# Count digits of a graph kernel stored in the order in which PE reads them

## The chip, the cores and the metric

The kernel runs on one core of a Trainium2 chip. The metric is the device time of one execution in microseconds (us). The engines are PE (matrix products; its weight loads are listed as PEld), DVE (vector), ACT (scalar), POOL (GpSimd) and SP, which here only issues DMAs. Each engine works through its own queue in order; marks on semaphores make one queue wait for another.

## The reference

Four graph layers over 8192 nodes of 32 features and 262144 edges, each followed by a residual and a layer norm. The edges come sorted by their target node `dst`.

```python
src = src[argsort(dst)]; dst = dst[argsort(dst)]
x = layernorm(x + segment_sum(einsum(x[src], weight[edge_type]), dst))   # 64 relations, 32 x 32 each
x = layernorm(x + segment_sum(x[src] * edge_weight[:, None], dst))
x = layernorm(x + segment_sum(x[src], dst))
x = layernorm(x + L3(x, src, dst, edge_attr_4, edge_attr_32, W1, b1, W2, b2, si_w0, si_w1))
```

Nothing in the reference counts edges. The kernel counts them because layers two and three work on matrices that are built from the edges of each node, and for that it has to find where each node's edges begin.

## The kernel before, in words

**Layout.** The 262144 edges stand as 2048 tiles of 128 edges, one edge per partition, so every per-edge array is 128 x 2048 (`TT` = 2048). Eight tiles (`GT` = 8) make a group; there are 256 groups (`GG`). The targets of a group lie in a window of 128 nodes that moves by 32 nodes per group, and `rel` is an edge's target within its window, 0 to 127.

**The first stage** (up to about 320 us) does two things at once. One is the table `ytab`: every node's features times all 64 relation matrices, 64 MB in memory. The loop at L391 makes it in 64 steps. A step is eight products on PE (L402), two copies out of the PSUM banks (L408, both on ACT at first, later one on ACT and one on DVE) and one store of 1 MB issued by SP (L410). Five buffers `ys` take turns, so a copy waits for the store of five steps ago.

The other thing is the start of every node's edges, in the generator `beginnings()` (L280). Each table step first advances the generator to its next `yield`, so the order of the queues is: what the generator issues, then the step's own table work. The generator runs as follows.

1. At its first turn it issues all digit work to DVE. L285 takes the target's position in the window, L286 to L289 split it into a low digit (0 to 15, `lo_b`) and a high digit (0 to 7, `hi_b`), both bf16 in the order of the edges: group, then tile within the group. L291 to L293 are checks and the conversion of `rel`. L296 makes the one-hot low digits `oh_lo`, one instruction for each of 16 values, stored as value x 2048 edges. L300 makes the one-hot high digits `oh_hi`, in two halves of eight instructions each; a mark `begun[h]` stands behind each half.
2. For 20 turns it does nothing, so 20 table steps are queued on PE.
3. In each of the next eight turns it queues count products for two blocks of 16 groups (L315 to L324). For each block and each of the eight tile positions `t`, one product multiplies the one-hot high digits of 16 groups (the weights, 128 columns: group x digit) with their one-hot low digits (the moving operand, 256 columns: digit x group), and the eight add up in PSUM bank 6. Only the parts in which both groups are the same are wanted: DVE multiplies with `mask` (L323) and sums over the group (L324). PE waits for `begun[0]` at the first turn, for `begun[1]` at the fifth, and at every turn for L324 of the turn before, since the bank is the same.
4. The counts are stored to `hist` (L327), read back shifted (L333), added up over the four windows in which a node can lie, and summed into running totals (L336 to L354).
5. POOL gathers 64 times the records of the edges with these totals as indices (the indirect DMAs of `laid_rec`).

**What follows.** POOL's gathers of `ytab` for the first layer wait for all stores of the table. Then come the first layer with the building of the matrices (to about 4835 us), the second and third layers, which read these matrices back (to about 5900 us), and the fourth layer.

**The lines of the change.** The moving operand is a view of `oh_lo` that takes, for a fixed tile position `t`, all 16 values and all 16 groups: from one column to the next the address moves by eight bf16 elements, 16 bytes, and from one value to the next by 2048 elements. The weights are a gapless run.

Of the kernel before, what the change touches and what calls it, by code (L numbers as in the profile page):

```python
# [13 lines left out]
BF = mybir.dt.bfloat16  # L14
I32 = mybir.dt.int32
AF = mybir.ActivationFunctionType
OP = mybir.AluOpType
# [4 lines left out]
P = 128  # L22
# [11 lines left out]
TT = E // P  # L34
GT = 8
# [110 lines left out]
def raw_layers(tc, x, a, w0, w1, b1, w2, si, m, bad):  # L146
    nc = tc.nc
    PE, V, A, G, S = (Flow(tc, e, n) for e, n in ((nc.tensor, "pe"), (nc.vector, "dve"), (nc.scalar, "act"),
                                                  (nc.gpsimd, "pool"), (nc.sync, "sp")))
    bank, arena = m["bank"], m["arena"]  # L150
# [33 lines left out]
    def own(f, ins):  # L184

        mk = f.mark(ins)
        f.after(mk)
        return mk
# [3 lines left out]
    cut = Carve()  # L192
# [13 lines left out]
    cut = Carve(8192)  # L206
    rg = cut(64, MS, 3)
    rgi = rg.rearrange("p a b c -> p (a b c)").bitcast(I32).rearrange("p (a b c) -> p a b c", b=MS, c=3)
    cut = Carve(8192)
    nxt = cut(TT, dt=I32)  # L210
    base = cut(GG, GT, dt=I32)
    cut = Carve()
    oh_lo = cut(16, TT, dt=BF)
    oh_hi = [cut(8, GT, 16, 8, dt=BF)]
    dg = cut
    dg4, pre, idx, idx2 = dg(4, 64), dg(2, 64), dg(64, dt=I32), dg(64, dt=I32)
    NY = 5
    ys = cut(NY, 4, 512)
    w0_s = cut(R * D)
    xT = cut(NB // 4, P)  # L220
    oh_hi.append(cut(8, GT, 16, 8, dt=BF))
    mask = cut(16, 16)
    c16 = cut(16, 16)
    ev = cut(2, 16, 16)
# [3 lines left out]
    hi_b = digits[:, 0:TT // 2].bitcast(BF)  # L228
    lo_b = digits[:, TT // 2:TT].bitcast(BF)
# [48 lines left out]
    begun = {}  # L278

    def beginnings():  # L280


        bf, xi = base.rearrange("p g t -> p (g t)"), x_a.rearrange("p d f -> p (d f)").bitcast(I32)
        V.after(dst_in, g2)
        own(V, V.e.tensor_tensor(bf, dsti, bf, op=OP.subtract))  # L285
        own(V, V.e.tensor_scalar(xi, bf, 15, None, op0=OP.bitwise_and))  # L286
        own(V, V.e.tensor_copy(lo_b, xi))
        own(V, V.e.tensor_scalar(xi, bf, 4, None, op0=OP.arith_shift_right))
        V.e.tensor_copy(hi_b, xi)  # L289
        V.after(nxt_in)  # L290
        own(V, V.e.tensor_tensor(nxt, dsti, nxt, op=OP.is_gt))  # L291
        V.e.tensor_reduce(ok[:, 2:3], nxt, AX.X, OP.max)
        own(V, V.e.tensor_copy(rel, bf))  # L293

        for c in range(16):
            V.e.tensor_scalar(oh_lo[:, c, :], lo_b, float(c), None, op0=OP.is_equal)  # L296
        for h in range(2):
            for k in range(8):
                t0 = 1024 * h + 128 * k
                ins = V.e.tensor_tensor(oh_hi[h][:, k].rearrange("p t g c -> p g t c"),  # L300
                                        m["iota_b"][:, None, None, 0:8].to_broadcast([P, 16, GT, 8]),
                                        hi_b[:, t0:t0 + 128].rearrange("p (g t) -> p g t", t=GT)[:, :, :, None].to_broadcast([P, 16, GT, 8]),
                                        op=OP.is_equal)
            begun[h] = V.mark(ins)
        S.after(zm)
        h_ld = Landing(tc, "st_hist")
        for g in (0, GG + 2):
            h_ld.add(S.e.dma_start(hist[g:g + 2].rearrange("g h c -> (g h) c"), z[0:8, 0:32].rearrange("p (h c) -> p h c", c=16)))
        for _ in range(20):
            yield  # L310
        V.after(g4)
        counts = bank[:, 6, :].rearrange("p (h c g) -> p h c g", h=2, g=16)
        cm = None
        for k in range(8):
            PE.after(begun[k // 4], cm)  # L315
            for h in range(2):
                n = 2 * k + h
                lv = oh_lo[:, :, 128 * n:128 * (n + 1)].rearrange("p c (g t) -> p c g t", t=GT)
                for t in range(GT):
                    ins = PE.e.matmul(counts[:, h], oh_hi[n // 8][:, n % 8, t].rearrange("p g c -> p (g c)"), lv[:, :, :, t],  # L320
                                      start=(t == 0), stop=(t == GT - 1))
            V.after(PE.mark(ins))
            own(V, V.e.tensor_tensor(ev, counts, mask[:, None].to_broadcast([P, 2, 16, 16]), op=OP.mult))  # L323
            cm = own(V, V.e.tensor_reduce(c16[:, 2 * k:2 * k + 2, :], ev, AX.X, OP.add))  # L324
            yield
        S.after(cm)
        hm = h_ld.add(S.e.dma_start(hist[2:GG + 2].rearrange("(s g) h c -> (g h) s c", s=16), c16))  # L327
        yield
        S.after(hm)
        d_ld = Landing(tc, "ld_deg")  # L330
        for i in range(4):
            v = hist[i:i + GG, 2 * (3 - i):2 * (3 - i) + 2, :].rearrange("(p b) h c -> p b (h c)", b=2)
            dm = d_ld.add(S.e.dma_start(dg4[:, i, :].rearrange("p (b n) -> p b n", b=2), v))  # L333
        yield
        V.after(dm)
        own(V, V.e.tensor_add(dg4[:, 0:2, :], dg4[:, 0:2, :], dg4[:, 2:4, :]))  # L336
        own(V, V.e.tensor_add(dg4[:, 2, :], dg4[:, 0, :], dg4[:, 1, :]))
        deg = dg4[:, 2, :]
        own(V, V.e.tensor_copy(pre[:, 0, :], deg))
        k = 1  # L340
        f = 0
        while k < 64:
            V.e.tensor_copy(pre[:, 1 - f, 0:k], pre[:, f, 0:k])
            own(V, V.e.tensor_add(pre[:, 1 - f, k:], pre[:, f, k:], pre[:, f, 0:64 - k]))
            k *= 2
            f = 1 - f
        vm = own(V, V.e.tensor_sub(pre[:, 1 - f, :], pre[:, f, :], deg))
        PE.after(vm, g3, cm)
        pm = PE.mark(PE.e.matmul(bank[:, 6, 0:1], upper, pre[:, f, 63:64], start=True, stop=True))
        V.after(pm)  # L350
        own(V, V.e.tensor_copy(small[:, 7:8], bank[:, 6, 0:1]))
        own(V, V.e.tensor_scalar(idx, pre[:, 1 - f, :], small[:, 7:8], None, op0=OP.add))
        own(V, V.e.tensor_scalar(idx2, idx, RG - 1, None, op0=OP.bitwise_and))
        im = own(V, V.e.tensor_scalar(idx, idx, RG.bit_length() - 1, None, op0=OP.arith_shift_right))  # L354

        G.after(im)
        r_ld = Landing(tc, "ld_rec")
        for k in range(64):
            begun["rec"] = r_ld.add(indirect(rg[:, k].rearrange("p s f -> p (s f)"), a["rec"], idx[:, k:k + 1]))
        yield  # L360

        own(V, V.e.tensor_tensor(pre[:, f, :], idx2, deg, op=OP.add))
        own(V, V.e.tensor_reduce(ok[:, 3:4], pre[:, f, :], AX.X, OP.max))
        V.after(src_in, row_in)
        begun["row"] = own(V, V.e.scalar_tensor_tensor(row, src, float(R), row, op0=OP.mult, op1=OP.add))
        V.e.tensor_reduce(ok[:, 0:1], rel, AX.X, OP.max)
        own(V, V.e.tensor_reduce(ok[:, 1:2], rel, AX.X, OP.min))
        own(V, V.e.tensor_scalar(ok[:, 0:1], ok[:, 0:1], float(P - 1), None, op0=OP.is_gt))
        own(V, V.e.tensor_scalar(ok[:, 1:2], ok[:, 1:2], 0.0, ok[:, 0:1], op0=OP.is_lt, op1=OP.max))
        own(V, V.e.tensor_scalar(ok[:, 2:3], ok[:, 2:3], 0.0, ok[:, 1:2], op0=OP.is_gt, op1=OP.max))  # L370
        om = V.mark(V.e.tensor_scalar(ok[:, 3:4], ok[:, 3:4], float(MS), ok[:, 2:3], op0=OP.is_gt, op1=OP.max))
        yield
        yield
        yield
        PE.after(om)
        pm = PE.mark(PE.e.matmul(bank[0:1, 6, 8:9], ok[:, 3:4], small[:, 1:2], start=True, stop=True))
        V.after(pm)
        own(V, V.e.tensor_copy(bad, bank[0:1, 6, 8:9]))
# [9 lines left out]
    n = 0  # L388
    rest = beginnings()
    busy = True  # L390
    for j in range(NB // 4):  # L391
        for c in range(4):
# [4 lines left out]
            for h in range(2):  # L397
# [3 lines left out]
                for q in (2 * h, 2 * h + 1):  # L401
                    ins = PE.e.matmul(bank[:, 2 * b + q % 2, :], xT[q * D:(q + 1) * D, j, :],  # L402
                                      w0_s[q * D:(q + 1) * D, c * 512:(c + 1) * 512], start=True, stop=True)
# [187 lines left out]
    for s in range(NS):  # L591
        if s == FIRST - 1:
            V.after(slots(), x_in)
        k, landed = gathers(ytab, row, s)
        g0 = s * WT // GT
        for h in range(2):
# [3 lines left out]
            for t in range(16):  # L600
                g = (s * WT + 16 * h + t) // GT
                bk = (g // per) % 2
                if t % GT == 0 and g % per == 0:
                    PE.after(agg_free[bk])
                c = g % per
                ins = PE.e.matmul(bank[:, bk, c * D:(c + 1) * D], oh[:, h, t, :], xg[:, k, 16 * h + t, :],  # L606
                                  start=(t % GT == 0), stop=(t % GT == GT - 1))
# [20 lines left out]
    cut = Carve()  # L628
# [47 lines left out]
    for n, (l, c) in enumerate(seq):  # L676
# [8 lines left out]
        for s in range(64):  # L685
            if l == 1:
                q = s % 4
                ins = PE.e.matmul(bank[q * D:(q + 1) * D, b, 0:256].rearrange("p (u h j) -> p u h j", h=2, j=4),  # L688
                                  x_b[:, s, :], mv[:, s], start=(s < 4), stop=(s >= 60), tile_position=(0, q * D))
            else:  # L690
                ins = PE.e.matmul(bank[0:96, b, 0:512].rearrange("p (u h j) -> p u h j", h=2, j=4),  # L691
                                  x3[:, s, :], mv[:, s], start=(s == 0), stop=(s == 63))
# [13 lines left out]
    cut = Carve()  # L706
# [20 lines left out]
    p = cut(NP, 4, MW)  # L727
# [110 lines left out]
    for q in range(NQ + 4):  # L838
# [3 lines left out]
        if q < NQ:  # L842
            k, wp = w_bank()
# [5 lines left out]
        c = q - 3  # L849
        if 0 <= c < NQ:  # L850
            g = c // 2
# [14 lines left out]
        ins = None  # L866
        if 0 <= q - 2 < NQ:
            c = q - 2
# [38 lines left out]
        c = q - 3  # L907
# [486 lines left out]
```

## Time and profile before

| what | us |
|---|---|
| median of three timed runs | 9409.51 |
| lowest and highest of them | 9387.47, 9425.49 |
| the profiled execution | 9317.46 |
| its span, first to last instruction | 9315.7 |
| PE busy, PE weight loads busy | 5952.4, 4149.0 |
| DVE, ACT, POOL busy | 3749.4, 1626.5, 3971.2 |
| count products L320, 128 of them, in a stage of | 75.0 |
| DVE: digits, from L285 to the end of L300 | 16.5 to 57.4 |

The shares of busy time are averages over stages with different limits. A weight load can run beside a product, so the two PE rows don't add up. [...]for the count products the start-to-start time is what counts, and it is read from the timeline. The granted clock is the share of its full rate that PE's throttle left it.

### The profile page before, as it was taken

The numbers are of one execution on the slowest core, as the hardware profiler recorded it, in microseconds if no ns is written. First come the engines' busy times: TensorE is split into PE (matmuls) and PEld (weight loads), VectorE is DVE, ScalarE is ACT, GpSimd is POOL, SyncE is SP. The second block draws the span as 40 slices with busy tenths as digits, with TensorE's granted clock in tenths as the row PEclk, the third lists the DMA queues.
The fourth block names the chain that finished last, engine by engine and source line by source line (L and its number), as shares of the span: only waits on it lengthen the run. The fifth ranks groups of instructions, "written<-read, shape, count | busy, mean of one in ns | idle before, by whom it ended". The sixth has DMA issues, their size and how long they took to land.

```text
span 9315.7 us, 88230 instructions
## 1 busy us (share of the span) xinstructions
PE 5952.4 (64%) x36084; PEld 4149.0 (45%) x36084; DVE 3749.4 (40%) x6576; ACT 1626.5 (17%) x2828; POOL 3971.2 (43%) x4174
## 2 busy tenths in 40 slices
PE   6325444544545445444464467399989988999899
PEld 2124444434445445444452234155555555555555
DVE  3213333333334333333330000166666665666666
ACT  3122222222222222222230000011111111111111
POOL 2554443443444444444400000655655555555551
PEclk6556666666666666666677778599998888989899
DMA  6304333333333333333369999011111110111110
GB/s 229 126 21 104 96 90 107 112 90 115 103 92 120 97 100 112 96 101 112 96 206 432 430 414 371 19 24 21 24 21 23 21 23 20 21 23 21 23 21 15
DMA packets 290653, 999.43 MB, mean 107 GB/s; under 512 B 98941, under 2 KB 175806, under 8 KB 250558
## 3 DMA queue, kind: packets, MB, share of 16 engines
q1 hardware_dynamic: 155662, 916.89, 27.3%
q0 software_dynamic: 134144, 73.67, 5.6%
q8 instruction: 285, 4.67, 0.2%
q10 hardware_dynamic: 432, 3.15, 0.1%
q14 instruction: 130, 1.06, 0.0%
HBM read 521.39 MB, written 471.99 MB: 107 GB/s over the span
## 4 chain that ended last, share of the span: by engine, by line
PE 38%; another core or an unknown queue 34%; DMA 15%; ACT 5%; issue 4%; DVE 3%; SPq 0%; ACTq 0%; DVEq 0%
PE bank L854 12%; PE bank L846 8%; DMA fcmat<-f_arena 7%; PE bank L828 5%; DMA f_arena<-famat 5%; PE bank L567 5%; PE bank L606 2%; DMA f_arena<-fcmat 2%; ACT f_arena L571 2%; ACT f_arena L572 2%; PE bank L688 2%; PE bank L691 1%; DVE f_arena L889 1%; PE bank L402 1%
## 5 line engine op out<-in xcount | busy, mean ns | idle before, releaser
L381 POOL DMA_INDIRECT f_arena<-fxtab,f_src x2048 | 1943.0, 949 | 2523.4 <-DMA fxtab<-f_x_b 1172.4
L381 POOL DMA_INDIRECT f_arena<-fytab,f_row x2048 | 1960.9, 957 | 2465.5 <-PE bank L606 1774.0
L567 PE MATMUL bank<-f_arena 64*128 64x128 f32 x16384 | 1382.4, 333 | 2109.5 <-ACT f_arena L572 1651.1
L567 PEld LDWEIGHTS bank<-f_arena 64*128 64x128 f32 x16384 | 1273.1, 238 | 2212.2 <-ACT f_arena L572 1667.5
L854 PE MATMUL bank<-f_arena 128*128 128x344 f32 x4096 | 1439.1, 498 | 165.7 <-DVE f_arena L501 127.1
L553 DVE TENSOR_TENSOR f_arena<-bank,f_arena 128x1024 f32<-128x1024 f32 x256 | 312.4, 1220 | 2557.9 <-PE bank L567 2490.5
L571 ACT ACTIVATE f_arena<-bank 128x512 bf16<-128x512 f32 x1024 | 612.9, 598 | 2928.0 <-remote 2204.8
L854 PEld LDWEIGHTS bank<-f_arena 128*128 128x128 f32 x4096 | 851.3, 210 | 602.0 <-DVE f_arena L501 157.4
L846 PE MATMUL bank<-f_arena 65*128 65x256 f32 x4096 | 1091.7, 412 | 0.0
L846 PEld LDWEIGHTS bank<-f_arena 65*128 65x128 f32 x4096 | 775.6, 199 | 538.2 <-issue 440.6
L833 ACT ACTIVATE f_arena<-bank,f_arena 64x512 f32<-64x512 f32 x512 | 350.3, 684 | 2913.2 <-PE bank L828 1475.6
L606 PE MATMUL bank<-f_arena 128*128 128x32 f32 x4096 | 686.9, 340 | 111.8 <-DMA f_arena<-fytab,f_row 59.6
L501 DVE TENSOR_TENSOR f_arena<-bank,f_rel 128x512 f32<-128x512 f32 (+1 forms) x640 | 634.5, 999 | 263.9 <-ACT f_arena L533 240.1
L606 PEld LDWEIGHTS bank<-f_arena 128*128 128x128 f32 x4096 | 679.9, 264 | 121.1 <-issue 115.5
L828 PE MATMUL bank<-f_arena 32*64 32x512 f32 x1024 | 577.4, 644 | 188.5 <-ACT f_arena L833 179.1
L572 ACT ACTIVATE f_arena<-bank 128x512 f32<-128x512 f32 x1024 | 611.3, 597 | 0.0
L882 DVE TENSOR_TENSOR f_arena<-bank,f_arena 128x256 f32<-128x256 f32 x512 | 216.1, 422 | 937.1 <-PE bank L846 379.1
L555 DVE TENSOR_TENSOR f_arena<-bank,f_arena 128x2048 f32<-128x2048 f32 x256 | 586.5, 2291 | 8.8
L889 DVE TENSOR_TENSOR f_arena<-bank,f_arena 128x256 f32<-128x256 f32 x1536 | 550.6, 414 | 0.0
L688 PE MATMUL bank<-f_arena,f_x_b 128*32 128x256 f32 x4096 | 295.5, 459 | 336.4 <-DMA f_arena<-famat 336.4
L688 PEld LDWEIGHTS bank<-f_arena,f_x_b 128*32 128x32 f32 x4096 | 145.6, 132 | 475.0 <-DMA f_arena<-famat 311.4
L885 DVE TENSOR_TENSOR f_arena<-bank,f_arena 128x512 f32<-128x512 f32 x512 | 348.6, 681 | 0.0
(127 smaller groups left out, 2711.9 us busy)
## 6 DMA issues: line engine op xcount, KB each, us to landing
famat<-f_arena SPq DMA_DIRECT2D x256, 1024.0 KB
fcmat<-f_arena SPq DMA_DIRECT2D x256, 512.0 KB
fytab<-f_arena SPq DMA_DIRECT2D x64, 1024.0 KB
f_arena<-fytab,f_row POOLq DMA_INDIRECT x2048
f_arena<-fxtab,f_src POOLq DMA_INDIRECT x2048
f_arena<-laid_ea SPq DMA_DIRECT2D x64, 512.0 KB
f_arena<-laid_ea SPq DMA_DIRECT2D x64, 64.0 KB
f_arena<-laid_xT ACTq DMA_DIRECT2D x1, 1024.0 KB, 8.3
```

Source lines behind the costliest of these rows:

```text
L381: return G.e.indirect_dma_start(out=dest, out_offset=None, in_=table, in_offset=bass.IndirectOffsetOnAxis(ap=ix, axis=0))
L501: return V.e.tensor_tensor(o, iota[:, None, :].to_broadcast([P, n, P]), rel[:, t:t + n, None].to_broadcast([P, n, P]), op=OP.is_equal)
L555: V.e.tensor_tensor(oh_l[:, b], iota[:, None, :].to_broadcast([P, 16, P]), meta_l[:, pp, k0:k0 + 16, None].to_broadcast([P, 16, P]), op=OP ...
L567: ins = PE.e.matmul(bank[:, bk + h, :].rearrange("p (c s j) -> p c s j", s=64, j=4)[:, :, :, j], oh_l[hs_, b, 4 * q + j, :], oh_k[hs_, b, ...
L571: A.e.activation(st_c[:, b, q], bank[:, bk:bk + 2, 0:256], AF.Copy)
L572: bank_free[units[0] % 2] = am = A.mark(A.e.activation(st_a[:, b, q], bank[:, bk:bk + 2, 256:512], AF.Copy))
L606: ins = PE.e.matmul(bank[:, bk, c * D:(c + 1) * D], oh[:, h, t, :], xg[:, k, 16 * h + t, :], start=(t % GT == 0), stop=(t % GT == GT - 1))
L688: ins = PE.e.matmul(bank[q * D:(q + 1) * D, b, 0:256].rearrange("p (u h j) -> p u h j", h=2, j=4), x_b[:, s, :], mv[:, s], start=(s < 4), ...
L828: pm = PE.mark(PE.e.matmul(bank[0:64, 2, :], w1_s[r * D:(r + 1) * D, :], ef[r * D:(r + 1) * D, k, (q % 8) // 4, :], start=True, stop=True))
L846: ins = PE.e.matmul(wp[:, t, :], hs[0:65, q % 3, t * P:(t + 1) * P], w2_s[0:65], start=True, stop=True)
L854: ins = PE.e.matmul(bank[:, g % 2, 0:MW], oh[:, c % NO, t, :], p[:, c % NP, t, :], start=(c % 2 == 0 and t == 0), stop=(c % 2 == 1 and t = ...
L889: V.e.tensor_tensor(pq[:, :, 128 + 64 * mm:192 + 64 * mm].rearrange("p t (o i) -> p t o i", i=8), wp[:, :, 192:256].rearrange("p t (o i) - ...
```

## The change

The order of the digits is changed where they are made, so that the count products read gapless runs. The casts of L287 and L289 write the digits in the order block of 16 groups, tile position, group, and read their int32 source with a step of eight elements to do so. `oh_lo` becomes (block and tile position) x value x group, so that each of the 16 comparisons writes 128 runs of 16 elements. `oh_hi` becomes (block and tile position) x group x digit, written gapless by one instruction per half in place of eight. The count products take one block of `oh_lo` and one of `oh_hi` at a time; their results stand in the bank as before, and L323's view of them is renamed accordingly. The sizes of the buffers, the marks and the order of the queues stay.

```diff
-    oh_lo = cut(16, TT, dt=BF)
-    oh_hi = [cut(8, GT, 16, 8, dt=BF)]
+    oh_lo = cut(16 * GT, 16, 16, dt=BF)
+    oh_hi = [cut(8 * GT, 16, 8, dt=BF)]
...
-    oh_hi.append(cut(8, GT, 16, 8, dt=BF))
+    oh_hi.append(cut(8 * GT, 16, 8, dt=BF))
...
-        own(V, V.e.tensor_copy(lo_b, xi))
+        own(V, V.e.tensor_copy(lo_b.rearrange("p (n t g) -> p n t g", t=GT, g=16),
+                               xi.rearrange("p (n g t) -> p n t g", t=GT, g=16)))
         own(V, V.e.tensor_scalar(xi, bf, 4, None, op0=OP.arith_shift_right))
-        V.e.tensor_copy(hi_b, xi)
+        V.e.tensor_copy(hi_b.rearrange("p (n t g) -> p n t g", t=GT, g=16),
+                        xi.rearrange("p (n g t) -> p n t g", t=GT, g=16))
...
         for c in range(16):
-            V.e.tensor_scalar(oh_lo[:, c, :], lo_b, float(c), None, op0=OP.is_equal)
+            V.e.tensor_scalar(oh_lo[:, :, c, :], lo_b.rearrange("p (k g) -> p k g", g=16), float(c), None, op0=OP.is_equal)
         for h in range(2):
-            for k in range(8):
-                t0 = 1024 * h + 128 * k
-                ins = V.e.tensor_tensor(oh_hi[h][:, k].rearrange("p t g c -> p g t c"),
-                                        m["iota_b"][:, None, None, 0:8].to_broadcast([P, 16, GT, 8]),
-                                        hi_b[:, t0:t0 + 128].rearrange("p (g t) -> p g t", t=GT)[:, :, :, None].to_broadcast([P, 16, GT, 8]),
-                                        op=OP.is_equal)
-            begun[h] = V.mark(ins)
+            n = 1024
+            begun[h] = V.mark(V.e.tensor_tensor(oh_hi[h].rearrange("p k g c -> p (k g) c"),
+                                                m["iota_b"][:, None, 0:8].to_broadcast([P, n, 8]),
+                                                hi_b[:, n * h:n * (h + 1), None].to_broadcast([P, n, 8]), op=OP.is_equal))
...
-        counts = bank[:, 6, :].rearrange("p (h c g) -> p h c g", h=2, g=16)
+        counts = bank[:, 6, :].rearrange("p (h n) -> p h n", h=2)
...
-                lv = oh_lo[:, :, 128 * n:128 * (n + 1)].rearrange("p c (g t) -> p c g t", t=GT)
                 for t in range(GT):
-                    ins = PE.e.matmul(counts[:, h], oh_hi[n // 8][:, n % 8, t].rearrange("p g c -> p (g c)"), lv[:, :, :, t],
+                    ins = PE.e.matmul(counts[:, h], oh_hi[n // 8][:, n % 8 * GT + t].rearrange("p g c -> p (g c)"),
+                                      oh_lo[:, n * GT + t].rearrange("p c g -> p (c g)"),
                                       start=(t == 0), stop=(t == GT - 1))
...
-            own(V, V.e.tensor_tensor(ev, counts, mask[:, None].to_broadcast([P, 2, 16, 16]), op=OP.mult))
+            own(V, V.e.tensor_tensor(ev, counts.rearrange("p h (c g) -> p h c g", g=16), mask[:, None].to_broadcast([P, 2, 16, 16]), op=OP.mult))
```

## The prediction, made before the changed kernel was run

> **What bounds the kernel now.** The change lies in the first 320 us, so I cut that stretch into stages with the view by windows (columns: stretch, its length, busy us of PE, PE's weight loads, DVE, ACT, POOL, granted clock, DMA share, GB/s):
>
> ```profile
> 17.00:64.50 47.50, 45.92 (x160) 16.56 (x152) 40.20 (x40) 36.54 (x39) 0.00 (x0) 0.72 1.03 392
> 64.50:139.50 75.00, 75.00 (x196) 20.04 (x196) 11.02 (x16) 15.27 (x16) 0.00 (x0) 0.50 0.44 162
> 139.50:166.00 26.50, 15.48 (x64) 6.28 (x58) 11.62 (x30) 13.24 (x14) 7.13 (x7) 0.59 0.62 201
> 166.00:248.00 82.00, 25.25 (x60) 6.22 (x56) 7.69 (x7) 7.58 (x9) 54.68 (x58) 0.53 0.54 182
> 248.00:318.00 70.00, 51.76 (x176) 18.50 (x176) 28.97 (x25) 23.27 (x23) 0.00 (x0) 0.57 1.00 362
> ```
>
> Before 64.5 us and after 248 us the stores of the table `ytab` fill the DMA engines (share 1.0). Between 64.5 and 139.5 us they don't (0.44, 162 GB/s): PE is busy without a gap, at half clock. That is the stage of the count products. The timeline shows one step of it:
>
> ```profile
> 64.58 7.41 PE L320 MATMUL bank<-f_arena 128*128 128x256 bf16 x16
> 71.92 2.09 PE L402 MATMUL bank<-f_arena 32*128 32x512 f32 x8
> 72.09 0.69 DVE L323 TENSOR_TENSOR f_arena<-bank,f_arena 128x512 f32<-128x512 f32 x1 [14.69 <-PE bank L320]
> 72.82 0.69 DVE L324 TENSOR_REDUCE f_arena<-f_arena 128x32 f32<-128x512 f32 x1
> 73.94 7.41 PE L320 MATMUL bank<-f_arena 128*128 128x256 bf16 x16
> ```
>
> From 64.58 to 73.94 a step takes 9.36 us: 16 count products (7.34 us, 0.459 each) and one step of the table (2.02 us). Eight of them are 74.9 us. Last, the chain of waits and the timeline say what hangs on their end:
>
> ```profile
> 141.98 5.43 DMA fhist<-f_arena
> 149.83 2.20 DMA f_arena<-fhist
> ```
> ```profile
> 157.04 1.10 POOL L381 DMA_INDIRECT f_arena<-laid_rec,f_arena  x1 [150.31 <-DVE f_arena L362]
> ...
> 318.56 0.94 POOL L381 DMA_INDIRECT f_arena<-fytab,f_row  x1 [80.51 <-DMA fytab<-f_arena]
> ```
>
> The counts go to memory and back, give the record gathers their indices at 157 us, and the first layer's gathers wait until the whole table is stored. PE holds the table back for 75 us, so time taken from the count products moves all that follows forward. Is a count product slow by its arithmetic? The third layer's bf16 products, later in the run, answer that:
>
> ```profile
> 5512.34 15.74 PE L691 MATMUL bank<-f_arena 128*96 128x512 bf16 x64 [3.73 <-DMA f_arena<-fcmat]
> ```
> ```profile
> 5516.00:5528.00 12.00, 12.00 (x57) 6.63 (x55) 0.00 (x0) 0.00 (x0) 0.00 (x0) 0.97 1.01 422
> ```
>
> 512 columns in 0.246 us at clock 0.97, loads hidden: 0.48 ns per column, so about 0.96 ns at half clock. The count product takes 1.79 ns per column. Its moving operand steps 16 bytes from one element to the next (`g`, `GT` = 8 bf16), while L691 reads runs of four neighbours.
>
> [...] PE is busy for all of 75 us here and stays at 0.50, so the busy row isn't the measure; L691's products read 0.97. [...]
>
> **The change, part by part.**
>
> *Count products* (L320, 128 of them). Moving operand and weights become gapless; columns, number and output stay. I take L691's rate: 0.246 us each at half clock, 0.123 at full. Bounds: 0.459 (the step was not the reason) and 0.123. Weight loads (0.126 mean, contiguous before too) stay under the product at half clock; exposed, a pair would take 0.37.
>
> *The step around them.* The next step's products wait for L323 and L324, which read the bank: from the last count product (71.92) to the next (73.94) is 2.02 us, and the table's eight products fill it. At half clock a step is 16 x 0.246 + 2.02 = 5.96 us. At full clock the table's products halve to about 1.05 and the wait on DVE ends last: 16 x 0.123 + 2.02 = 3.99 us. Both stay above the 2.57 us in which a step's megabyte is stored (ACT's copies start at 53.69, 56.25 and 58.81), so the gain isn't cut by the DMA.
>
> *Digits on DVE.* DVE's rows:
>
> ```profile
> 20.07 1.23 DVE L287 CAST f_x_b<-x_a 128x2048 bf16<-128x2048 int32 x1
> 22.60 1.23 DVE L289 CAST f_x_b<-x_a 128x2048 bf16<-128x2048 int32 x1
> 29.51 9.73 DVE L296 TENSOR_SCALAR f_arena<-f_x_b 128x2048 bf16<-128x2048 bf16 x16
> 39.16 18.25 DVE L300 TENSOR_TENSOR f_arena<-f_iota_b,f_x_b 128x1024 bf16<-128x1024 bf16 x16
> ```
>
> The two casts now read int32 at 32-byte steps. Bounds: 1.23 (nothing lost; a gain is excluded, they were contiguous) and 4.2 times that, the worst strided access in this trace (ACT's L533 writes 512 elements at a step in 2.54 us, L571 without one in 0.60): +3.9 each. I take 2.29[...]: +2.1 for both. The 16 comparisons that make `oh_lo` now write runs of 16 elements (32 bytes) with gaps. Bounds: 0.61[...] and 2.29 each, +26.9 in all[...]. I take 0.61[...]. For `oh_hi`, 16 instructions become two of 8192 elements: 2.29 for the first 2048 (L285) and 1.07 per further 1024 (2.29 less L300's 1.22) give 8.7 each, 17.4 against 18.25. A doubled rate would give 4.4; I exclude slower, since the rows of eight are as before.
>
> So the first half of `oh_hi` is ready at 29.5 + 2.1 + 9.7 + 8.7 = 50.0 us, the second at 58.7. PE asks for the first at 64.58 and for the second four steps later: 14.6 us of cover, the table's first 20 steps, and more for the second. With casts and comparisons at their upper bounds the first is ready at 29.5 + 7.8 + 36.6 + 8.7 = 82.6 us, 18 us late, and then the queue of PE stands still with the table's products behind it.
>
> *Evictions* (L323, L324) see the same bank layout: nothing. SP's queue keeps its order (table stores, then the counts' store, then four loads); all come sooner, with stores still spaced wider than 2.57 us ahead of them. I keep 5.43 and 2.20 us. The 64 record gathers (80 us), the slow table steps beside them, and the 2.57 us steps until 306 us move forward whole.
>
> *Sum.* Two steps at half clock, six at full: 2 x 5.96 + 6 x 3.99 = 35.9 us against 74.9: -39 us. The profiled execution took 9317.5 us (span 9315.7): 9278.5. It is 92 us under the median of the timed runs (9409.5); I carry the difference over: 9370.
>
> **Rivals.**
> A, the forecast: gapless products, and the dense stream is granted full clock: 9370. For: L691. Against: this stage shows 0.50 throughout. Chance 0.45.
> B: the products speed up but the clock stays at half: 8 x 5.96 = 47.7, gain 27, 9382. For: table steps at half clock with 2.09 of 2.57 us busy never raised it between 39 and 64 us. 0.33.
> C: PE's step isn't the limit (weight loads or a fixed cost per product): gain 0 to 10, 9405. Against: L691. 0.07.
> D: [...] 18 us late, 39 - 18 = 21 gained, 9388. 0.09.
> E, slower: the gaps only move from PE's reads to DVE's writes. If a gapped bf16 write costs what ACT's L533 pays, 4.96 ns per element, a comparison takes 10.2 us and `oh_lo` 163 us; the first half of `oh_hi` is ready near 209 us, PE stands 144 us, and less the 39 gained the time is 9514. It turns slower once `oh_hi` is ready later than 64.6 + 39 = 104 us, which with slow casts is 3.5 us per comparison. Against: [...] L533 writes single elements. 0.06.
>
> **How the numbers follow.** About 0.5%, 47 us, is what a measurement tells from no change. The three runs spread over 38 us, so I give a case's median a spread of 25. Faster by over 47: 0.18 from A (its 39 lies just under), 0.07 from B, 0.01 from the others: 0.26. Slower: E and a tail of C: 0.08. Within: 0.66. The range, 9330 to 9418, takes in A and B with their spread, D and most of C; E and the tails, some 0.15, stay outside.
>
> **What would show it.** L320 at 0.25 or 0.12 us each in place of 0.46, and the granted clock of that stage, tell A from B from C. L296 spaced 0.61 or 2.3 us tells D and E; PE waiting for DVE ahead of its first count product would be their mark. The first record gather should start near 118 us (A) or 130 us (B), and the first table gather near 280 or 292 us. If it doesn't move with them, the table's stores were the bound after all, and the forecast is wrong.

## The result, and the profile after

| what | before | after |
|---|---|---|
| median of 20 timed runs, us | 9417.4 | 9376.6 |
| lowest and highest of them | 9372.67, 9457.12 | 9353.98, 9410.4 |
| the profiled execution | 9317.46 | 9368.31 |
| eight count steps, first product to end of the last | 72.9 | 27.9 |
| first record gather on POOL | 157.04 | 110.91 |
| first table gather on POOL | 318.56 | 275.49 |

The ratio of the times is 0.9959, with a 95% interval of 0.9946 to 0.9971. The medians differ by 41 us, and the interval stands for 27 to 51 us. (The ratios in this document are those on record for the timed runs; the quotient of two medians can differ a little, here 0.9957.) The profiled execution of before was an unusually quick one, below the lowest of its 20 timed runs, so the two spans must not be subtracted. What can be compared is the first 320 us. The rest of the run, from the first table gather to the end, took 8997 us in the profile of before and 9091 us in that of after, and between 9039 and 9088 us in eleven others of kernels that are alike in that part.

The timeline of PE in the changed kernel (start us, busy us, engine, line, operation, tiles, shape, how many; in brackets the idle time ahead and what ended it). L318 are the count products, L401 the table's:

```profile
64.28 3.47 PE L318 MATMUL bank<-f_arena 128*128 128x256 bf16 x16
67.68 1.14 PE L401 MATMUL bank<-f_arena 32*128 32x512 f32 x8
69.33 1.92 PE L318 MATMUL bank<-f_arena 128*128 128x256 bf16 x16 [0.51 <-DVE f_arena L323]
71.18 1.14 PE L401 MATMUL bank<-f_arena 32*128 32x512 f32 x8
72.82 1.92 PE L318 MATMUL bank<-f_arena 128*128 128x256 bf16 x16 [0.51 <-DVE f_arena L323]
...
90.31 1.92 PE L318 MATMUL bank<-f_arena 128*128 128x256 bf16 x16 [0.51 <-DVE f_arena L323]
```

From start to start (a product alone is listed with 273 ns, median, so the listed durations overlap): sixteen products take 3.40 us in the first step (0.2125 each), 1.85 in the second (0.116), where they took 7.34. A step takes 5.05 us once and 3.49 after that, where it took 9.36. PE now waits half a microsecond for DVE ahead of each group of products; before it never waited here (75.00 us busy in a stage of 75.00).

The view by windows (stretch, its length, then busy us of PE, PE's weight loads, DVE, ACT and POOL, granted clock, DMA share, GB/s):

```profile
17.00:64.00 47.00, 45.04 (x156) 16.19 (x151) 40.64 (x26) 36.23 (x39) 0.00 (x0) 0.71 1.03 393
64.00:96.00 32.00, 28.20 (x206) 16.05 (x204) 11.02 (x16) 18.14 (x19) 0.00 (x0) 0.95 1.03 378
96.00:112.00 16.00, 4.34 (x20) 1.98 (x18) 4.72 (x23) 3.27 (x5) 1.09 (x1) 0.57 0.69 218
```

The stage of the count products reads a clock of 0.95 in place of 0.50, and its DMA share 1.03 in place of 0.44: the table's stores no longer run dry beside them. In the third window PE is nearly idle while the counts go to memory and back.

DVE's timeline, the digits first and then the two operations that follow each step's products:

```profile
19.89 2.02 DVE L287 CAST f_x_b<-x_a 128x2048 bf16<-128x2048 int32 x1
23.21 2.02 DVE L290 CAST f_x_b<-x_a 128x2048 bf16<-128x2048 int32 x1
30.92 9.72 DVE L298 TENSOR_SCALAR f_arena<-f_x_b 128x2048 bf16<-128x2048 bf16 x16
40.56 17.28 DVE L301 TENSOR_TENSOR f_arena<-f_iota_b,f_x_b 128x8192 bf16<-128x8192 bf16 x2
...
71.36 0.69 DVE L322 TENSOR_TENSOR f_arena<-bank,f_arena 128x512 f32<-128x512 f32 x1 [2.09 <-PE bank L318]
72.08 0.69 DVE L323 TENSOR_REDUCE f_arena<-f_arena 128x32 f32<-128x512 f32 x1
```

The comparisons for `oh_lo` write with gaps at the rate at which they wrote without (0.61 us each in both profiles, from 9.72 and 9.73 us for sixteen). The first half of `oh_hi` is ready at 49.2 us, 15 us before PE asks for it.

The way behind the products, from the chain of waits and POOL's timeline:

```profile
95.75 5.86 DMA fhist<-f_arena
...
103.71 2.21 DMA f_arena<-fhist
```
```profile
110.91 1.10 POOL L380 DMA_INDIRECT f_arena<-laid_rec,f_arena  x1 [104.20 <-DVE f_arena L361]
...
275.49 0.94 POOL L380 DMA_INDIRECT f_arena<-fytab,f_row  x1 [83.75 <-DMA fytab<-f_arena]
```

Store and load of the counts nearly keep their length (5.43 and 2.20 us before). The record gathers start 46.1 us earlier, the table gathers 43.1 us, and that is the saving.

### The profile page after: what moved, and what is told of

The parts are those of the page before. It is cut to its first block, busy times and chain, and to the rows that moved or that the text cites. A ratio compares the mean times of both kernels' runs of the same rounds, so it can differ in the third digit from the quotient of the medians.

```text
span 9366.6 us, 88216 instructions
## 1 busy us (share of the span) xinstructions
PE 5968.9 (64%) x36084; PEld 4185.4 (45%) x36084; DVE 3748.9 (40%) x6562; ACT 1626.4 (17%) x2828; POOL 3965.5 (42%) x4174
## 4 chain that ended last, share of the span: by engine, by line
another core or an unknown queue 35%; PE 35%; DMA 15%; DVE 6%; ACT 5%; issue 4%; SPq 0%; ACTq 0%; DVEq 0%
PE bank L853 11%; PE bank L845 8%; DMA fcmat<-f_arena 7%; DMA f_arena<-famat 5%; PE bank L566 5%; PE bank L827 5%; DMA f_arena<-fcmat 2%; ACT f_arena L570 2%; ACT f_arena L571 2%; PE bank L687 2%; PE bank L605 2%; PE bank L690 1%; DVE f_arena L888 1%; DVE f_arena L500 1%
## 5 line engine op out<-in xcount | busy, mean ns | idle before, releaser
L853 PE MATMUL bank<-f_arena 128*128 128x344 f32 x4096 | 1487.3, 511 | 216.1 <-DVE f_arena L500 168.4
L853 PEld LDWEIGHTS bank<-f_arena 128*128 128x128 f32 x4096 | 873.4, 216 | 679.7 <-DVE f_arena L500 202.3
L605 PEld LDWEIGHTS bank<-f_arena 128*128 128x128 f32 x4096 | 696.1, 270 | 132.9 <-issue 127.7
```

The lines of the kernel that those rows point to most:

```text
L853: ins = PE.e.matmul(bank[:, g % 2, 0:MW], oh[:, c % NO, t, :], p[:, c % NP, t, :], start=(c % 2 == 0 and t == 0), stop=(c % 2 == 1 and t = ...
```

## The experiments

In all of them the marker is the time from the first count product to the first table gather: 254.0 us before, 211.2 in the profile of after and 208.3 in a second profile of it. The rest of the run scatters by tens of microseconds and hides a few.

**1. Only the low digits, or only the high ones.** Which of the two operands made the products slow? The first kernel keeps the new order of `oh_lo` and makes `oh_hi` with the 16 instructions of before, the second is the reverse.

```diff
# relative to the changed kernel
...
-            begun[h] = V.mark(V.e.tensor_tensor(oh_hi[h].rearrange("p k g c -> p (k g) c"), ...
+            for k in range(8):
+                ins = V.e.tensor_tensor(oh_hi[h][:, k * GT:(k + 1) * GT].rearrange("p t g c -> p g t c"), ...
+            begun[h] = V.mark(ins)
```
```diff
# relative to the kernel before
...
+            begun[h] = V.mark(V.e.tensor_tensor(oh_hi[h].rearrange("p k t g c -> p (k t g) c"), ...
```

> Only the low digits take the new order; the high digits are made by the 16 instructions of before. Theory S (the step of the moving operand is the cause): count products 0.12 us each at full clock, stage of the count products 28 us as after the change, first gather of the table near 275.5 us (277 at most), ratio to before 0.994 to 0.998. Theory D (the gain comes from DVE's shorter digit work): products stay at 0.46 us, first gather near 318 us, ratio 1.000.

> Only the high digits take the new order and the two long instructions; the low digits are as before. Theory S: products 0.46 us, clock 0.50, stage 75 us, first gather of the table 318 us within 2, ratio 1.000 within 0.0015. Theory D: the first gather moves to about 275 us, ratio 0.996.

PE's timeline with only the low digits, then the window of the products with only the high digits:

```profile
62.84 3.59 PE L320 MATMUL bank<-f_arena 128*128 128x256 bf16 x16
...
71.50 1.92 PE L320 MATMUL bank<-f_arena 128*128 128x256 bf16 x16 [0.51 <-DVE f_arena L325]
```
```profile
62.00:135.00 73.00, 73.00 (x186) 18.76 (x184) 9.65 (x14) 15.50 (x16) 0.00 (x0) 0.50 0.45 169
```

Low digits alone: products as after, marker 209.7 us, time 9355.25 against 9385.42, ratio 0.9953 (0.9938 to 0.9969; the quotient of these medians is 0.9968). High digits alone: 0.457 us per product at clock 0.50 as before, marker 254.4 us, ratio 1.0004 (0.9993 to 1.0016). The whole effect is the order of the moving operand. The long `oh_hi` instructions save DVE one microsecond where nothing waits for it.

**2. What in that order was slow.** The moving operand of before had two marks: a step of 16 bytes, and after every 16 columns a jump to the next value. In the next three kernels T of the eight tile positions stand innermost, which gives one uniform step of 2 x T bytes and no jump. The casts and comparisons on DVE are rewritten to make that order.

```diff
# relative to the changed kernel; T = 8, 4, 2 and TH = 8 / T
-    oh_lo = cut(16 * GT, 16, 16, dt=BF)
+    oh_lo = cut(16 * TH, 16, 16 * T, dt=BF)
...
-                                      oh_lo[:, n * GT + t].rearrange("p c g -> p (c g)"),
+                                      oh_lo[:, n * TH + t // T].rearrange("p c (g l) -> p (c g) l", l=T)[:, :, t % T],
```

> The block order of the change, but with the eight tile positions innermost, so that the moving operand has one uniform step of 16 bytes over all 256 columns; no jump between values is left. Theory S[...]: products 0.46 us, clock 0.50, first gather of the table near 318 us. Rival J (the pattern with two dimensions and its jump of 4096 bytes between values is the cause, not the step): products 0.12 us, first gather near 276 us.

> Four tile positions innermost: a uniform step of 8 bytes[...]. [...] products 0.12 us and full clock, first gather near 276 us. If the cost grows with the bytes passed over: products between, about 0.23 us at half clock or slower, first gather near 290 us.

> Two tile positions innermost: a uniform step of 4 bytes[...]. [...] products 0.12 us, full clock, first gather of the table near 276 us. If the cost grows with the bytes passed over: above 0.12 us, but under the run with 8 bytes.

PE's timeline with 16 bytes, 8 bytes and 4 bytes, one fence each:

```profile
73.08 7.41 PE L317 MATMUL bank<-f_arena 128*128 128x256 bf16 x16
```
```profile
62.64 3.79 PE L320 MATMUL bank<-f_arena 128*128 128x256 bf16 x16
66.36 1.14 PE L403 MATMUL bank<-f_arena 32*128 32x512 f32 x8
68.00 3.79 PE L320 MATMUL bank<-f_arena 128*128 128x256 bf16 x16 [0.51 <-DVE f_arena L325]
71.72 1.14 PE L403 MATMUL bank<-f_arena 32*128 32x512 f32 x8
```
```profile
71.68 1.99 PE L320 MATMUL bank<-f_arena 128*128 128x256 bf16 x16 [0.51 <-DVE f_arena L325]
73.59 1.14 PE L403 MATMUL bank<-f_arena 32*128 32x512 f32 x8
```

For comparison, the first step in a second profile of the changed kernel, whose clock reads 0.50 from 64.16 to 67.68 us:

```profile
64.16 3.59 PE L318 MATMUL bank<-f_arena 128*128 128x256 bf16 x16
67.68 1.58 PE L401 MATMUL bank<-f_arena 32*128 32x512 f32 x8
```

And the windows of the 8-byte kernel, around its first two steps:

```profile
62.00:66.00 4.00, 4.00 (x17) 1.87 (x16) 0.00 (x0) 1.94 (x2) 0.00 (x0) 0.52 1.03 382
68.00:72.00 4.00, 4.00 (x20) 2.00 (x24) 0.10 (x1) 1.47 (x2) 0.00 (x0) 1.00 1.03 380
```

The step alone does it: 16 bytes without a jump cost what before did (marker 254.1 us). With 8 bytes, sixteen products take 3.72 us, and the pairs 62.64 to 66.36 and 68.00 to 71.72 are equal, although the windows read a clock of 0.52 around the first and 1.00 around the second. So the clock doesn't set this pace. Divided by 16 x 256 columns:

| step | ns per column | columns per 16 bytes | ns per 16 bytes |
|---|---|---|---|
| 16 bytes | 1.79 | 1 | 1.79 |
| 8 bytes | 0.91 | 2 | 1.82 |
| 4 bytes | 0.47 | 4 | 1.87 |
| gapless, clock 1.00 | 0.45 | 8 | 3.6 |
| gapless, clock 0.50 | 0.86 | 8 | 6.9 |

The rows with 16 and 8 bytes fit one price, some 1.8 ns for each 16 bytes passed. That a product takes whichever is longer, this price or PE's own pace (0.45 ns per column at clock 1.00, 0.86 at 0.50), is an estimate from these five rows. The 4-byte row can't tell the two apart. Steps above 16 bytes were not run. The markers follow: 222.9 us with 8 bytes, 208.7 with 4. For 8 bytes the second expectation gave the right time per product (0.2325 us), but not the half clock that it went with. At half clock 8 bytes cost little more than no gaps (0.91 ns beside 0.86), at clock 1.00 about twice as much as 4 bytes or no gaps (0.91 beside 0.47 and 0.45). The first expectation's 0.12 us per product was missed with 8 bytes; with 4 bytes it came true (0.119).

**3. Is PE still the bound?** One kernel issues each count product twice. The other issues one of eight, so it leaves seven eighths of the edges out of the counts, and its record gathers read other places.

```diff
-                for t in range(GT):
+                for t in (*range(GT), *range(GT)):
```
```diff
-                for t in range(GT):
+                for t in range(1):
...
-                                      start=(t == 0), stop=(t == GT - 1))
+                                      start=(t == 0), stop=True)
```

> The changed kernel with every count product issued twice (the second pass starts the sum anew). The stage grows by 128 x 0.12 = 15.4 us. Theory P (PE still holds the table back one for one): first gather of the table near 291 us. Theory H (the stores are now the bound of that stage and hide PE's work): 276 to 281 us.

> The changed kernel with one of eight count products per block: 7/8 of the edges are left out of the counts, so the positions of the records are wrong. 112 x 0.12 = 13.4 us less PE work. Theory P: first gather of the table near 263 us. Theory H: 270 to 275 us, since the stores already fill the DMA engines in that stage.

PE's timeline with doubled products, then the chain of waits with an eighth of them:

```profile
69.87 3.67 PE L318 MATMUL bank<-f_arena 128*128 128x256 bf16 x32 [0.50 <-DVE f_arena L323]
...
75.11 3.67 PE L318 MATMUL bank<-f_arena 128*128 128x256 bf16 x32 [0.51 <-DVE f_arena L323]
```
```profile
73.57 11.73 DMA fytab<-f_arena
...
88.08 12.02 DMA fhist<-f_arena
...
102.14 2.08 DMA f_arena<-fhist
```

Doubled: a step is 5.24 us, 1.75 more, the first one 2.3 more, 14.5 us in eight steps, and the marker moves by 11 to 14 us (to 222.55). Above the present level PE's time counts nearly one for one. An eighth: the steps take 2.1 to 3.1 us, 2.6 on average, which is the pace of the stores, and from 73.57 us the chain runs through the table's stores. The counts' store takes 12.02 us in place of 5.86; the DMA share is 1.03 from 64 to 96 us. So the record gathers begin 46.2 us after the first count product, against 46.6 in the changed kernel. The marker falls by only 3 to 6 us (to 205.57), where taking PE's time at full worth would have given 13.4. In its first three steps a pair of products is listed with 0.61 us, against 0.39 from the fifth on, so the clock was still low and PE's part longer there, and the other places of its records may bear on the rest. With that said, below the present level the stores become the bound: the change has taken most of what shorter count products can give in this stage.

**4. The gap behind the products.** In the changed kernel PE's timeline has a hole while the counts go to memory and back:

```profile
94.41 2.96 PE L401 MATMUL bank<-f_arena 32*128 32x512 f32 x12 [0.27 <-ACT f_arena L407]
109.03 0.59 PE L348 MATMUL bank<-f_arena,f_upper 128*128 128x1 f32 x2 [11.66 <-DVE f_arena L346]
```

PE's queue is in order, and L348, which sums the counts, stands ahead of the table's next steps. Four more turns of the generator put four table steps ahead of it.

```diff
+        yield
+        yield
+        yield
+        yield
         V.after(dm)
```

> The changed kernel with four more turns between the loads of the shifted counts and the work that waits for them, so that four table steps run on PE, ACT and the DMA engines while the counts are on their way. Theory F (the gap of 12 us in PE's queue is lost to the table): first gather of the table 8 to 10 us earlier, near 267 us, ratio to before 0.994 to 0.996. Rival: the record gathers start later by what the table gains, first gather near 275 us.

PE's timeline in that kernel at the same place, its window there, and POOL's first table gather:

```profile
92.39 10.29 PE L405 MATMUL bank<-f_arena 32*128 32x512 f32 x44 [0.27 <-ACT f_arena L411]
107.79 0.59 PE L352 MATMUL bank<-f_arena,f_upper 128*128 128x1 f32 x2 [5.11 <-DVE f_arena L350]
```
```profile
96.00:112.00 16.00, 10.89 (x46) 4.28 (x46) 5.97 (x23) 9.93 (x11) 2.02 (x2) 0.82 0.90 297
```
```profile
260.12 0.95 POOL L384 DMA_INDIRECT f_arena<-fytab,f_row  x1 [69.42 <-DMA fytab<-f_arena]
```

The record gathers don't come later (109.68 us), the table gathers come sooner than the expected 267 us, and the marker falls to 197.7 us, 11 below the nearer of the two profiles of after. To set the whole times beside each other, the changed kernel and this one ran once more on one chip:

> The changed kernel itself, beside the next run on the same chip. From the first count product to the first gather of the table 208 to 212 us, ratio to before 0.994 to 0.998; if the extra 3 us between the record gathers and the table gathers in its first profile belong to the kernel, 211 us again, otherwise near 209.

> The kernel with four table steps in the gap, beside the changed kernel on one chip. Theory F: 11 to 13 us ahead of the changed kernel at the first gather of the table, and 0.001 to 0.0015 below it in the ratio to before, which the intervals may not part.

| kernel | median, us | before, same chip | ratio | 95% interval | marker |
|---|---|---|---|---|---|
| filled, first | 9317.53 | 9380.34 | 0.9936 | 0.9923 to 0.9949 | 197.7 |
| changed, again | 9339.38 | 9381.03 | 0.9960 | 0.9947 to 0.9972 | 208.3 |
| filled, again | 9329.47 | 9381.03 | 0.9950 | 0.9932 to 0.9968 | 198.3 |

The marker moves by 10 us both times. Between the two last rows the whole times differ by 10 us too, but the scatter allows anything from -2 to 20 (an estimate from the 13 and 8 runs), so the ten microseconds of the filled kernel are shown in the first stage and not in the total. Both kernels are faster than before.

**5. Starting the count products earlier.** The products waited through 20 table steps while their first digits were ready some 15 us ahead. This kernel takes 14 in place of 20, with the gap filled.

```diff
# relative to the filled kernel
-        for _ in range(20):
+        for _ in range(14):
```

> As the kernel with four table steps in the gap, but with 14 table steps ahead of the count products in place of 20. Digits: PE meets the end of DVE's first half of the high digits, so the first count product starts at 49 to 50 us and PE waits for DVE there. Theory T (the table needs its bytes and its slow stretch beside the record gathers, wherever these lie): record gathers start near 97 us, first gather of the table near 260 us as before. Rival (the record gathers lead the table): 247 us.

PE's timeline, DVE's, the window of the products and the first table gather:

```profile
48.67 3.60 PE L318 MATMUL bank<-f_arena 128*128 128x256 bf16 x16 [1.50 <-DVE f_arena L301]
...
58.60 3.59 PE L318 MATMUL bank<-f_arena 128*128 128x256 bf16 x16 [4.92 <-DVE f_arena L323]
```
```profile
39.93 17.29 DVE L301 TENSOR_TENSOR f_arena<-f_iota_b,f_x_b 128x8192 bf16<-128x8192 bf16 x2
57.13 0.69 DVE L322 TENSOR_TENSOR f_arena<-bank,f_arena 128x512 f32<-128x512 f32 x1
```
```profile
62.00:90.00 28.00, 25.19 (x179) 13.24 (x178) 9.65 (x14) 17.35 (x19) 0.00 (x0) 0.98 0.71 261
```
```profile
269.76 0.94 POOL L384 DMA_INDIRECT f_arena<-fytab,f_row  x1 [86.36 <-DMA fytab<-f_arena]
```

The first product came at 48.67 us and waited for L301, as expected to within half a microsecond; that is how the cover of the digits ends. Both theories on the table missed: its gathers start at 269.76 us, 8 to 10 us later than in the two profiles of the filled kernel. The second step waited 4.92 us for L323: DVE works in order, and the first step's L322 and L323 stood behind the second half of `oh_hi`. During this hole PE fed the table nothing, and the clock fell back: the table's eight products before it took 1.48 us (2.09 at clock 0.50 in the kernel before, 1.14 at 1.00), the second step's sixteen took 3.52 us again, as at 0.50. The record gathers came at 102.53 us in place of 97. The stores ran dry: the DMA share is 1.02 from 17 to 62 us and 0.71 from 62 to 90, beside the products, where the second profile of the filled kernel has 1.03. A reckoning that fits, and that no run tested alone: six table steps fewer stand ahead of the record gathers, 15.4 us at 2.57 us each, while these gathers gained only 7 to 8 us on the filled kernel's. That leaves about 8 us, and 8 to 10 were measured.

## Why the prediction was right

The forecast was 39 us less; 41 (27 to 51) came, and 9376.6 us lies 6.6 above the predicted time. That distance says little: the forecast stood on a median of three runs, 8 us below that of twenty. It is chance, too, that the totals lie only 2 us apart: the first stage alone gave 43 to 46 us by the marker, and rival B's gain of 27 us lies at the edge of the interval. So the prediction is judged by its steps.

- **The mechanism: the step between elements makes a product slow.** Right, and shown by the first two experiments: the low digits alone do it, and a uniform step of 16 bytes without a jump costs the same as before. How the prediction read the excess was wrong. It set the 1.79 ns against 0.96 ns, PE's pace at half clock (1.87 times), as if the penalty came on top of the clock; the 8-byte kernel shows a pace that doesn't move with the clock (1.82 ns for each 16 bytes, at 0.52 and 1.00 alike). If that pace holds for a 16-byte step too, the stage of before would have been as slow at full clock; no run had a high clock with that step. Rival C, a fixed cost per product or the weight loads, falls at 0.116 us per product.
- **Clock.** Forecast A against its rival B: the dense stream is granted a high clock, 0.95 over the stage. The forecast leaned that way by 0.45 to 0.33 with one later product (L691) to go by, so this was a good guess more than a finding. "Two steps at half clock" was one too many; the second step already ran at 0.116 us per product (2.5 us less than summed).
- **Product.** At full clock 0.123 us was taken and 0.116 measured. At half clock, 0.246 was taken, against 0.220 in the second profile (clock 0.50 throughout) and 0.2125 in the first, where the clock rose before the step's end. The 0.246 was doubled from a product at clock 0.97; the measured 0.116, doubled, would also be too much.
- **The wait for DVE, the term that was mis-sized.** The sum kept 2.02 us between the last product of a step and the first of the next, read from the kernel before, and said that at full clock "the wait on DVE ends last". It does, but the 2.02 us were the length of the table's products that covered it. The chain itself is 71.18 to 72.82: 1.64 us, made of L322 and L323 (0.69 each) and the marks between. The lines shown with the prediction held it already: L324 is over at 73.51 us, 0.43 before the next product. A wait behind a cover was taken at the length of its cover. A full-clock step came out at 3.49 in place of 3.99: 0.38 of this is the wait, 0.12 the sixteen products. Over six steps that is 3.0 us. Together with the clock of the second step (2.5) and the first step (0.9), that is the difference between the 35.9 us of the sum and the 29.5 measured for the eight steps.
- **Digits on DVE.** Right in each of its choices, to within 0.3 us. Casts 2.02 us (2.29 taken), comparisons 0.61 with gaps (0.61 taken, the author's estimate: the profile of before showed it without gaps only), the long `oh_hi` instructions 17.28 us (17.4). The halves were ready at 49.2 and 57.8 us (50.0 and 58.7). The kernel with 14 steps shows that the cover was real and where it ends. The slower rival E and its milder form D (comparisons at 2.29 us each) fall.
- **What hangs behind.** Record gathers near 118 us, table gathers near 280: measured 110.9 and 275.5. The counts' way through memory nearly kept its length (5.86 and 2.21 us for 5.43 and 2.20), and the rest moved forward whole. In that one profile the stretch from record to table gathers was 3 us longer than in before or in its own second profile.
- **That "the gain isn't cut by the DMA".** It held, with little to spare: a step of 3.49 us against stores every 2.57, so 0.9 us per step was left. The kernel with an eighth of the products ran into the stores.

Left open: what makes the table steps beside POOL's record gathers slow was not tried, and the point from which PE's clock rises was not isolated. A stream with a 16-byte step stayed at 0.50 through 73 us without a gap, one with 8 bytes was granted 1.00 from its second step on (68 to 72 us).

## What to carry to other kernels

When a product's time per column is far above that of another product in the same trace (here 1.79 ns beside 0.48), look at the byte step of its moving operand first, and try to spend the reordering where the data is made: here rows of 32 bytes cost the comparisons nothing (0.61 us each as before), and the casts' step of 32 bytes 0.8 us each (2.02 for 1.23). Before a covered wait is put into a sum, add up the wait itself from its instructions; the length of what covers it is only an upper bound. And once a stage moves, ask what the next queue can take: here the stores' 2.57 us per step lay so close below that PE's remaining time was worth less than half its length.

## What the runs showed of the hardware

- A moving operand in bf16 (128 x 256) cost some 1.8 ns for every 16 bytes passed: 1.79 at a step of 16 bytes, 1.82 at 8, the latter at clock 0.52 and 1.00 alike. Without gaps the time followed the clock (0.45 ns per column at 1.00, 0.86 at 0.50); at 4 bytes (0.47 at 1.00) the two lie too close together to tell.
- A busy PE row alone didn't raise the clock: the products with a 16-byte step read 0.50 through 73 us of unbroken work. With gapless products it rose: with the first of them at 64.28 us the clock was 0.50 until 67 us and 1.00 from 67.7. In other profiles it came sooner (first product at 63.15 us, sixteen in 2.80 us) or later (first product at 64.16 us, 0.50 until 67.68, sixteen in 3.52 us).
- A cast on DVE that reads int32 at steps of 32 bytes took 2.02 us for 128 x 2048 elements, against 1.23 without gaps.
